# Writing p to DRAM straight from its 128x8 block on ScalarE's queue, in a two-layer graph attention kernel

## The chip, the cores and the metric

One core of one Trainium2 chip runs the kernel in one launch. The metric is the device time of a run in microseconds (us). Beside it stands the span of the profiled execution: the time from its first to its last instruction. The engines are TensorE (PE, with its weight loads as PEld), VectorE (DVE), ScalarE (ACT), GpSimd (POOL) and SyncE (SP, which only issues transfers here).

## The reference, cut to what matters

There are 16 graphs ("batches") of 1,024 nodes with 256 features, and a 0/1 matrix `adj` for each. Two layers follow each other. The second one needs, for each node, a few numbers that are shared with all other nodes:

```
# layer 0
x = layernorm(x + sigmoid(where(adj==1, leaky((x*a0) @ x.T), -inf)) @ x + bias)
# layer 1
Hh = x @ W;  s = Hh @ a_src;  d = Hh @ a_dst
e  = where(adj != 0, exp(-leaky_relu(s[:,None] + d[None,:])), 0)
x  = layernorm(x + elu((e @ Hh) / rowsum(e)))
```

The kernel does not compute `e` by an exponential for each pair of nodes. It makes exponentials for each node, p and q, and one VectorE instruction then makes a row tile of weights as min(p of the column times q of the row, adj). For that, q is wanted with one number per partition, as it comes, and p is wanted as a row of 1,024 numbers that is the same on all 128 partitions. p arrives in the other shape: `pq_kept[:, 0:8]`, 128 partitions by 8 tiles of nodes. Turning the one shape into the other is what is changed here.

## The kernel before, in words

A batch is handled in eight tiles of 128 nodes. The loop `for b in range(1, B)` works on layer 0 of batch b and on layer 1 of batch `prev` = b - 1 at the same time, and finishes the norm of batch `done` = b - 2. There is no scheduler that moves instructions: each engine executes its instructions in the order in which they are written, and a wait on an engine holds up all that is written behind it on that engine.

The first part of the loop body is a loop over eight strips (`jt`). In each of them

- `strip(b, jt)` makes the scores of the strip's nodes with the nodes at or right of them: TensorE matmuls into `pe` (L254), two tanh on ScalarE (L262, L263), a maximum on VectorE (L264). `finish` (L270) writes the result into `al`. Scores left of the diagonal are not computed, since the score matrix is symmetric.
- `dump(b, jt)` turns the strip by VectorE's 32x32 transposes (L290) and writes it to DRAM with four transfers on SP's queue (L294, `mir<-tb`). `gather(b, t)` reads strip t back, mirrored, into `al` (L298, `al<-mir`). In SP's queue they stand in this order: dump 0, dump 1, gather 0, dump 2, gather 1, dump 3, gather 2, gather 3, dump 4, dump 5, gather 4, dump 6, gather 5, gather 6. `mask(b, t, ...)` multiplies what gather t has brought by `adj` on VectorE (L305).
- `project(prev, t)` makes H and the numbers p and q of one tile of nodes of the batch before: two matmuls (L582), then on ScalarE three small exponentials and products; the third of them (L594) writes the tile's columns of `pq_kept`. The larger copy of H out of PSUM (L603) is put off until the next tile, and `evict_H` does the last one. Tiles 6 and 7 are projected in strip 4.

In strip 5 the products of layer 0 begin. They follow Strassen's scheme with seven half-size products (L477). `product(b, 1)` is put ahead of strip 5's scores and needs only unmirrored parts. `product(b, 5)`, four matmul steps ahead of strip 6's scores, needs the top left quarter of `al`, mirrored, masked and combined. VectorE prepares it in this order: mask 0 and combine rows 0 and 1 (written in strip 4); then in strip 5 mask 1 and combine row 2 (`combine_al(b, 1, 2, 3)`, L455), the lower halves of masks 0 and 1, mask 2 and combine row 3 (`combine_al(b, 1, 3, HT)`). Each of the four steps of the product reads one of the four rows. After the strips come products 3, 6, 7, 2 and 4, then the weights of the batch before (L643, `e`) and its sums (L648).

`share_p(prev)` stands in strip 5 right behind `product(b, 1)`. TensorE transposes the 128x8 block into PSUM (L610), ScalarE copies the 8x128 result to SBUF (L612), GpSimd's queue writes it to DRAM in eight runs of 512 B (L614, `p_row<-row`), and the same queue, after that has landed, reads it back to all 128 partitions (L616, `p<-p_row`). Behind these on GpSimd is `center` of batch `done` (L338 to L374), whose results `mr` and `r` ScalarE needs for scaling `y_kept` (L379).

The last batch is done in two halves by `share_half`: VectorE transposes `pq_kept` by 32x32 blocks (L624), GpSimd's queue writes four transfers (L628) and reads the half back (L629).

Transfers tell their landing by semaphores. The built program has eight of them for the transfers that SP and ScalarE issue, given out in rotation over both queues, in an order that the builder makes of the engines' lists and that is not the order of time on the chip, and eight others for GpSimd's. A transfer whose semaphore is still out waits on its own queue until the earlier transfer with the same semaphore has landed.

Of the kernel before, what the change touches and what calls it, by code (L numbers as in the profile page):

```python
# [9 lines left out]
F32 = mybir.dt.float32  # L10
# [8 lines left out]
P = 128  # L19
HALF = 512  # L20
BIG = 1.0e30
SLOPE = 0.2
SQ = 32
# [7 lines left out]
def one_kind_pass(  # L31
# [33 lines left out]
    nc = tc.nc  # L65
    B, N, D = x.shape
    NT = N // P
    ND = D // P
    HT = HALF // P
# [6 lines left out]
    one = ctx.enter_context(tc.tile_pool(name="one", bufs=1))  # L76
    two = ctx.enter_context(tc.tile_pool(name="two", bufs=2))
    dram = ctx.enter_context(tc.tile_pool(name="dram", bufs=2, space=bass.MemoryType.DRAM))
# [521 lines left out]
    def evict_H():  # L600

        for H, acc, wr in unscaled:
            nc.scalar.mul(H, acc, wr)  # L603
        unscaled.clear()

    def share_p(b):


        pt = ps_t.tile([P, HT, P], F32, tag="t", name=f"prow_{b}")[0:NT, 0, :]
        nc.tensor.transpose(pt, pq_kept[:, 0:NT], ident)  # L610
        row = one.tile([NT, P], F32, tag="row", name=f"row_{b}")
        nc.scalar.copy(row, pt)  # L612
        p_row = dram.tile([N], F32, tag="p_row", name=f"p_row_{b}")
        nc.gpsimd.dma_start(p_row.rearrange("(t p) -> t p", p=P), row)  # L614
        p_bcs[b] = one.tile([P, N], F32, tag="p", name=f"p_{b}")
        nc.gpsimd.dma_start(p_bcs[b], p_row.partition_broadcast(P))  # L616

    def share_half(b, t0):


        if t0 == 0:
            p_bcs[b] = one.tile([P, N], F32, tag="p", name=f"p_{b}")
        pT = one.tile([P, SQ], F32, tag="pT", name=f"pT_{b}_{t0}")
        nc.vector.transpose(pT, pq_kept)  # L624
        p_row = dram.tile([HALF], F32, tag="p_half", name=f"p_row_{b}_{t0}")
        v = p_row.rearrange("(t i j) -> i t j", i=P // SQ, j=SQ)
        for i in range(P // SQ):
            nc.gpsimd.dma_start(v[i], pT[ds(i * SQ + t0, HT), :])  # L628
        nc.gpsimd.dma_start(p_bcs[b][:, ds(t0 * P, HALF)], p_row.partition_broadcast(P))  # L629

    def check_pq(b):
        near = small.tile([P, 2, NT], F32, tag="near", name=f"near_{b}")
# [148 lines left out]
    for b in range(1, B):  # L781
        prev, done = b - 1, b - 2
        last = b == B - 1

        projects = [[0, 1], [2], [3], [4, 5], [6, 7], [], [], []]
        if prev == 0:

            projects = [[], [], [0, 1], [2, 3], [4, 5, 6, 7], [], [], []]
        for jt in range(NT):
            if jt == 4:  # L790
                mask(b, 0, 0, HT)
                combine_al(b, 1, 0, 2)
            if jt == 5:
                new_yT(b)
                product(b, 1)
                share_p(prev)
                mask(b, 1, 0, HT)
                combine_al(b, 1, 2, 3)
                mask(b, 0, HT)
                mask(b, 1, HT)  # L800
                mask(b, 2, 0, HT)
                combine_al(b, 1, 3, HT)
                mask(b, 2, HT)
                if done >= 0:
                    r1s[done] = center(mv1s[done], f"1_{done}", unit=1.0 / D)
            if jt == 6:
                unite(b, "p1")
                product(b, 5)
                unite(b, "p5")
                combine_al(b, 2, 0, HT)  # L810
            strip(b, jt)
            if jt == 5:
                mask(b, 3, HT)
            finish(b, jt, ends=False)
            if jt == 4:
                gather(b, 3)
            if jt < NT - 1:
                dump(b, jt)
            if jt < 2 and done >= 0:
                deviation1(done, NT - 2 + jt)  # L820
            if prev == 0 and jt == 0:
                turn_x1(0, 0)
            if prev == 0 and jt == 1:
                transpose_x1(0)
            if jt >= 1 and jt != 4:
                gather(b, jt - 1)
            if jt < 4 and b == 1:
                combine_x(b, jt)
            for t in projects[jt]:
                project(prev, t)  # L830
            if jt == 4:
                evict_H()
            add_twice(b, jt)
        if not last:
            new_xT(b + 1)
            load_blocks(xTs[b + 1], x[b + 1], 0, N)

        def extras(n):
            if prev == 0 and n < 2:
                scale0(0, HT + 2 * n)  # L840
                scale0(0, HT + 2 * n + 1)
            elif prev > 0:
                scale0(prev, 2 * n)
                scale0(prev, 2 * n + 1)
            if done >= 0:
                for q in (2 * n, 2 * n + 1):
                    scale1(done, q)
                    if q == 3:
                        store(done, 0, HT)
            if n < 3:  # L850
                check_adj(b, n)

        product(b, 3)
        combine_al(b, 3, 0, HT)
        extras(0)
        product(b, 6)
        weights(prev, 0)
        mask(b, 4)
        mask(b, 5)
        combine_al(b, 4, 0, 2)  # L860
        mask(b, 6)
        combine_al(b, 4, 2, HT)
        unite(b, "u2")
        extras(1)
        product(b, 7)
        extras(2)
        product(b, 2)
        extras(3)
        unite(b, "s")
        unite(b, "c12")  # L870
        unite(b, "c22")
        unite(b, "c11")
        product(b, 4)
        turn_y(b, 0)
        if done >= 0:
            store(done, HT, HT)
        weights(prev, 1)
        weights(prev, 2)
        weights(prev, 3)
        weights(prev, 4)  # L880
        unite(b, "c21")
        turn_y(b, 1)
        fetch_y(b, 0)
        fetch_y(b, 1)
        if not last:
            load_x(b + 1, [nc.sync])
        check_adj(b, 3)
        weights(prev, 5)
        weights(prev, 6)
        weights(prev, 7)  # L890
        check_pq(prev)
        if not last:
            load_adj(b + 1, 0, behind=x1s[b][:, HT, 0:1])

        def sum_of(t):
            homes = {"a": (ps_acc, "acc"), "e": (ps_e, "e"), "t": (ps_t, "t")}
            return acc1(prev, t, *homes[("aaeteeaa" if last else "aaeettat")[t]])

        n_first = 3
        first = [sum_of(t) for t in range(n_first)]  # L900
        for m in range(NT):
            for t in range(n_first):
                sum1(prev, t, first[t], m)
        if not last:
            turn_x(b + 1, 0, False)
            turn_x(b + 1, 1, False)
        rinvs = invert_sums(prev, first)
        for t in range(NT):
            if t >= n_first:
                acc = sum_of(t)  # L910
                for m in range(NT):
                    sum1(prev, t, acc, m)
            if last and t == 7:
                for m in range(4):
                    weights(b, m, 0, HT)
            elu(prev, t, *((first[t], rinvs[t]) if t < n_first else (acc,)))
            if last and t in (2, 3):
                for q in range(HT):
                    stats0(b, (t - 2) * HT + q)
                roots0(b, t - 2)  # L920
            if t >= 1:
                add(prev, t - 1)
            if t >= 2:
                deviation1(prev, t - 2)
            if not last and t in (3, 5):
                sums0(b, (t - 3) // 2)
                if t == 5:
                    load_adj(b + 1, 1, behind=mv0s[b][:, HT, 0:1])
            if not last and t >= 4:
                for q in range(2 * t - 8, 2 * t - 6):  # L930
                    deviation0(b, q)
                if t % 2 == 1:
                    roots0(b, (t - 5) // 2)
            for n in ([0], [1], [2, 3])[t - 5] if not last and t >= 5 else []:
                combine_x(b + 1, n)
            if t == 3 and not last:
                scale_x(b + 1, 0)
                scale_x(b + 1, 1)
            if last and t in (4, 6):
                t0 = (t - 4) // 2 * HT  # L940
                for n in range(HT):
                    project(b, t0 + n)
                evict_H()
                share_half(b, t0)
            if last and t in (5, 7):
                for q in range(HT):
                    scale0(b, (t - 5) // 2 * HT + q)
            if last and t == 7:
                for m in range(4, 6):
                    weights(b, m, 0, HT)  # L950
        if not last:
            add(prev, NT - 1)
# [522 lines left out]
```

## Time and profile before

| what | value |
|---|---|
| time, median of 3 runs | 1219.08 us (1217.61 to 1219.70) |
| profiled execution, its own time | 1218.96 us |
| its span | 1217.2 us |
| PE busy | 1206.9 us (99%), 4,400 matmuls |
| PEld, DVE, ACT, POOL busy | 67%, 82%, 70%, 32% |
| granted TensorE clock | 0.998 of full |
| transfers | 604,600 packets, 180.66 MB, 56.0% of the 16 engines' time by the queue that SP uses |

The profiled execution is 0.12 us under the median of the runs. Between two batches lie 74.4 us. A busy share is a share of the whole span; a wait names the instruction that waited, and behind the arrow what released it. "Landing" is the time at which a transfer's semaphore was raised.

### The profile page before, as it was taken

How to read it: one execution, taken by the hardware profiler on the slowest of the kernel's cores; microseconds unless marked ns; L12 is line 12 of the kernel's file. 1: busy time of each engine (PE TensorE's matmuls, PEld its weight loads, DVE VectorE, ACT ScalarE, POOL GpSimd, SP SyncE). 2: the span in 40 equal slices, each digit the busy share in tenths (PEclk: the TensorE clock that was granted, in tenths of full speed). 3: DMA queues.
4: the chain of work that ended last, by engine and by line, in shares of the span. 5: the costliest groups of instructions: out<-in, count | busy, mean ns of one | idle time of the engine just before them, and what ended most of it. 6: DMA issues, size and time to landing. Idle time of an engine off the chain costs nothing.

```text
span 1217.2 us, 15868 instructions
## 1 busy us (share of the span) xinstructions
PE 1206.9 (99%) x4400; PEld 819.4 (67%) x4400; DVE 993.4 (82%) x1759; ACT 846.5 (70%) x2150; POOL 391.2 (32%) x730
## 2 busy tenths in 40 slices
PE   9999999999999999999999999999999999999997
PEld 6757657576575866758667585775757657576686
DVE  5698797887969789797897978879798796887957
ACT  4574867767687676867768677786776867577674
POOL 3320333404243142441414324143340433404243
PEclk9999999999999999999999999999999999999999
DMA  9568787797878878788787886877769787887512
GB/s 195 104 133 153 130 158 154 148 184 137 154 152 155 180 136 160 145 166 172 142 171 132 156 179 132 176 139 143 173 143 189 128 156 151 156 182 137 112 52 73
DMA packets 604600, 180.66 MB, mean 148 GB/s; under 512 B 482012, under 2 KB 586968, under 8 KB 604504
## 3 DMA queue, kind: packets, MB, share of 16 engines
q1 hardware_dynamic: 582800, 136.90, 56.0%
q0 software_dynamic: 21008, 42.01, 18.8%
q8 instruction: 37, 0.61, 0.2%
q10 hardware_dynamic: 696, 0.66, 0.2%
q14 instruction: 59, 0.48, 0.1%
HBM read 152.44 MB, written 60.62 MB: 175 GB/s over the span
## 4 chain that ended last, share of the span: by engine, by line
PE 96%; ACT 2%; DVE 1%; POOL 1%; DMA 0%; issue 0%; ACTq 0%; DVEq 0%; POOLq 0%
PE acc L648 36%; PE pe L254 20%; PE pH L582 9%; PE pQ L477 8%; PE pV L477 8%; PE pW L477 8%; PE pR L477 4%; PE acc L396 2%; ACT junk L130 0%; ACT y_kept L379 0%; DMA p_row<-row 0%; PE busy L149 0%; PE pal L313 0%; ACT x L379 0%; POOL ve L338 0%
## 5 line engine op out<-in xcount | busy, mean ns | idle before, releaser
L648 PE MATMUL acc<-H,e 128*128 128x257 f32 x2032 | 445.6, 380 | 0.6 <-DVE e L643 0.6
L648 PEld LDWEIGHTS acc<-H,e 128*128 128x128 f32 x2032 | 384.8, 190 | 64.8 <-issue 7.2
L254 PE MATMUL pe<-xa,xT 128*128 128x384 f32 (+1 forms) x720 | 249.5, 486 | 0.2 <-DVE xa L235 0.2
L254 PEld LDWEIGHTS pe<-xa,xT 128*128 128x128 f32 x720 | 132.8, 190 | 90.0 <-issue 50.7
L284 POOL TENSOR_TENSOR al<-ident,al 128x128 f32<-128x128 f32 x128 | 103.7, 818 | 198.6 <-DVE al L270 198.5
L643 DVE SCALAR_TENSOR_TENSOR e<-p,pq_kept,adj 128x1024 f32<-128x1024 f32 (+1 forms) x136 | 159.2, 1224 | 0.0
L455 DVE TENSOR_TENSOR al<-al 128x1024 f32<-128x1024 f32 (+2 forms) x105 | 144.9, 1380 | 11.7 <-POOL al L284 4.5
L264 DVE TENSOR_TENSOR tb<-tb,low 128x512 f32<-128x512 f32 (+1 forms) x192 | 104.7, 551 | 39.8 <-ACT low L263 39.7
L262 ACT ACTIVATE tb<-pe 128x512 f32<-128x512 f32 (+1 forms) x192 | 93.8, 489 | 59.4 <-PE pe L254 57.7
L130 ACT ACTIVATE junk<-adj,minus 128x2048 bf16<-128x2048 bf16 x64 | 127.3, 1990 | 0.0
L582 PE MATMUL pH<-Wx,yT 128*128 128x258 f32 x480 | 116.3, 380 | 0.0
L104 POOL CAST adj<-x 128x1 bf16<-128x1 f32 x15 | 3.2, 212 | 348.9 <-DMA x<-y_rows 298.4
L582 PEld LDWEIGHTS pH<-Wx,yT 128*128 128x128 f32 x480 | 91.2, 190 | 31.1 <-issue 13.4
L477 PE MATMUL pV<-al,S 128*128 128x512 f32 x240 | 107.9, 592 | 0.0
L477 PE MATMUL pW<-al,x 128*128 128x512 f32 x240 | 107.9, 592 | 0.0
L477 PE MATMUL pQ<-al,x 128*128 128x512 f32 x240 | 107.9, 592 | 0.0
L270 DVE SCALAR_TENSOR_TENSOR al<-tb,adj 128x512 f32<-128x512 f32 (+7 forms) x132 | 97.4, 739 | 4.5
L305 DVE SCALAR_TENSOR_TENSOR al<-al,adj 128x512 f32<-128x512 f32 (+3 forms) x150 | 81.6, 564 | 18.6 <-DMA al<-mir 18.1
L263 ACT ACTIVATE low<-pe 128x512 f32<-128x512 f32 (+1 forms) x192 | 94.1, 490 | 1.2 <-DVE tb L264 1.2
L379 ACT ACTIVATE y_kept<-y_kept,mr,r 128x256 f32<-128x256 f32 x120 | 64.9, 588 | 42.9 <-POOL mr L374 41.7
L674 ACT ACTIVATE sums<-acc,tiny 128x1 f32<-128x1 f32 x45 | 11.7, 261 | 111.0 <-PE acc L648 111.0
L684 DVE TENSOR_SCALAR rinv<-acc 128x1 f32<-128x1 f32 x82 | 12.8, 157 | 89.9 <-PE acc L648 89.8
(152 smaller groups left out, 1681.7 us busy)
## 6 DMA issues: line engine op xcount, KB each, us to landing
adj<-in_adjT POOLq DMA_DIRECT2D x30, 1024.0 KB, 8.4
x<-in_x SPq DMA_DIRECT2D x15, 1024.0 KB
y_rows<-Z SPq DMA_DIRECT2D x240, 64.0 KB, 2.0
x<-y_rows SPq DMA_DIRECT2D x30, 512.0 KB, 4.3
out<-y_kept SPq DMA_DIRECT2D x30, 512.0 KB, 3.0
xT<-in_x SPq DMA_DIRECT2D x112, 128.0 KB, 4.0
p<-p_row POOLq DMA_DIRECT2D x15, 512.0 KB, 4.2
mir<-tb SPq DMA_DIRECT2D x60, 112.0 KB, 3.0
```

The costliest lines, as they stand in the source:

```text
L130: nc.scalar.activation(junk, rows, AF.Square, bias=minus1, scale=2.0, accum_out=chk[:, b * CHECKS + n : b * CHECKS + n + 1],)
L254: nc.tensor.matmul(pe[:, 0:w], lhsT=xTs[b][:, c, ts(jt, P)], rhs=xas[b][:, c, ds(jt * P + o, w)], start=(c == 0), stop=(c == ND - 1),)
L262: nc.scalar.activation(tb[:, ds(o, w)], pe[:, 0:w], AF.Tanh, scale=0.5)
L263: nc.scalar.activation(low[:, 0:w], pe[:, 0:w], AF.Tanh, scale=0.5 * SLOPE)
L264: nc.vector.tensor_tensor(tb[:, ds(o, w)], tb[:, ds(o, w)], low[:, 0:w], ALU.max)
L270: nc.vector.scalar_tensor_tensor(als[b][:, jt, c0:c1], tbs[b, jt][:, c0 - jt * P : c1 - jt * P], 1.0, adjs[b, jt // HT][:, jt % HT, c0:c1] ...
L284: nc.gpsimd.tensor_tensor(diag, ident2, diag, ALU.add)
L455: nc.vector.tensor_tensor(out_, in0, in1, ALU.subtract)
L477: nc.tensor.matmul(banks[bank], lhsT=lhs[:, jt, :], rhs=rhs[:, jt, :], start=first and jt == 0, stop=jt == HT - 1, skip_group_check=True,)
L582: nc.tensor.matmul(pt, lhsT=x1Ts[b][:, c, ts(t, P)], rhs=Wx[:, c, :], start=(c == 0), stop=(c == ND - 1),)
L643: nc.vector.scalar_tensor_tensor(e, p_bcs[b][:, cols], q, rows, ALU.mult, ALU.min)
L648: nc.tensor.matmul(acc, lhsT=es[b][:, m, ts(t, P)], rhs=Hs[b][m], start=(m == 0), stop=(m == NT - 1),)
```

## The change

ScalarE writes p to DRAM itself, out of the 128x8 block, with one transfer in which every number is an element of its own: 1,024 elements of 4 B, since neighbours in a partition lie 512 B apart in DRAM. This stands in strip 4, between the exponentials of the last tile and the last copy of H. TensorE's transpose, ScalarE's copy and GpSimd's write go. GpSimd's read back to all partitions keeps its place. In the last batch the two halves are written in the same way, 512 elements each, and VectorE's transpose and the four writes of each half go.

```diff
-    def share_p(b):
-        pt = ps_t.tile([P, HT, P], F32, tag="t", name=f"prow_{b}")[0:NT, 0, :]
-        nc.tensor.transpose(pt, pq_kept[:, 0:NT], ident)
-        row = one.tile([NT, P], F32, tag="row", name=f"row_{b}")
-        nc.scalar.copy(row, pt)
-        p_row = dram.tile([N], F32, tag="p_row", name=f"p_row_{b}")
-        nc.gpsimd.dma_start(p_row.rearrange("(t p) -> t p", p=P), row)
-        p_bcs[b] = one.tile([P, N], F32, tag="p", name=f"p_{b}")
-        nc.gpsimd.dma_start(p_bcs[b], p_row.partition_broadcast(P))
-
-    def share_half(b, t0):
+    p_rows = {}
+
+    def save_p(b, t0, n):
+        p_rows[b, t0] = dram.tile([n * P], F32, tag=f"p_row_{n}", name=f"p_row_{b}_{t0}")
+        with nc.allow_non_contiguous_dma(reason="a column per tile of nodes"):
+            nc.scalar.dma_start(
+                p_rows[b, t0].rearrange("(t p) -> p t", p=P), pq_kept[:, ds(t0, n)]
+            )
+
+    def share_p(b, t0, n):
         if t0 == 0:
             p_bcs[b] = one.tile([P, N], F32, tag="p", name=f"p_{b}")
-        pT = one.tile([P, SQ], F32, tag="pT", name=f"pT_{b}_{t0}")
-        nc.vector.transpose(pT, pq_kept)
-        p_row = dram.tile([HALF], F32, tag="p_half", name=f"p_row_{b}_{t0}")
-        v = p_row.rearrange("(t i j) -> i t j", i=P // SQ, j=SQ)
-        for i in range(P // SQ):
-            nc.gpsimd.dma_start(v[i], pT[ds(i * SQ + t0, HT), :])
-        nc.gpsimd.dma_start(p_bcs[b][:, ds(t0 * P, HALF)], p_row.partition_broadcast(P))
+        nc.gpsimd.dma_start(
+            p_bcs[b][:, ds(t0 * P, n * P)], p_rows[b, t0].partition_broadcast(P)
+        )
...
             if jt == 5:
                 new_yT(b)
                 product(b, 1)
-                share_p(prev)
+                share_p(prev, 0, NT)
...
             for t in projects[jt]:
                 project(prev, t)
             if jt == 4:
+                save_p(prev, 0, NT)
                 evict_H()
...
                 for n in range(HT):
                     project(b, t0 + n)
+                save_p(b, t0, HT)
                 evict_H()
-                share_half(b, t0)
+                share_p(b, t0, HT)
```

## The prediction

> **What bounds the kernel now.** I read the page first, then the waits, then one steady batch (6) engine by engine in the timeline, then the transfers. From the page, the engines' busy time and the chain that ended last:
>
> ```profile
> PE 1206.9 (99%) x4400; PEld 819.4 (67%) x4400; DVE 993.4 (82%) x1759; ACT 846.5 (70%) x2150; POOL 391.2 (32%) x730
> PE 96%; ACT 2%; DVE 1%; POOL 1%; DMA 0%; issue 0%; ACTq 0%; DVEq 0%; POOLq 0%
> ```
>
> TensorE is the bound. A change gains only what it takes from TensorE's own list, and loses whatever makes TensorE wait. From the waits, by engine:
>
> ```profile
> POOL p L616 <- DMA p_row<-row: 40.5, 15, 3.7
> ACT row L612 <- PE prow L610: 28.0, 15, 2.1
> DVE al L305 <- DMA al<-mir: 18.1, 18, 1.6
> PEld acc L648 <- DVE e L643: 2.1, 4, 1.0
> ```
>
> The path of p is made of waits (lines 1 and 2), but on engines that aren't the bound. VectorE waits for gathers (line 3), so it has no time in hand before strip 5's masks. TensorE's own losses are four short stalls (line 4). Now batch 6, the timelines of PE, ACT and POOL:
>
> ```profile
> 451.23 0.27 PE L610 MATMUL prow<-ident,pq_kept 128*8 128x128 f32 x1
> 451.34 1.46 PE L254 MATMUL pe<-xa,xT 128*128 128x384 f32 x4
> 452.63 3.60 PE L477 MATMUL pV<-al,S 128*128 128x512 f32 x8
> ...
> 448.72 0.25 ACT L594 ACTIVATE pq_kept<-pH,rcol 128x2 f32<-128x2 f32 x1
> 448.86 0.83 ACT L603 ACTIVATE H<-pH,wr 128x256 f32<-128x256 f32 x2
> ...
> 452.09 0.63 POOL L614 DMA_DIRECT2D p_row<-row  x1 [1.56 <-ACT row L612]
> 455.50 0.57 POOL L616 DMA_DIRECT2D p<-p_row  x1 [2.79 <-DMA p_row<-row]
> ```
>
> The transpose holds TensorE from 451.23 to 451.34. The p numbers are complete at 448.97 (448.72 + 0.25). The same batch on SP's queue and on VectorE:
>
> ```profile
> 446.54 0.44 SPq L298 DMA_DIRECT2D al<-mir  x1
> 447.03 2.26 SPq L294 DMA_DIRECT2D mir<-tb  x4
> 449.70 2.59 SPq L298 DMA_DIRECT2D al<-mir  x2
> ...
> 450.53 0.38 DVE L305 SCALAR_TENSOR_TENSOR al<-al,adj 128x256 f32<-128x256 f32 x1
> 453.23 0.29 DVE L305 SCALAR_TENSOR_TENSOR al<-al,adj 128x128 f32<-128x128 f32 x1 [0.31 <-DMA al<-mir]
> 453.62 0.69 DVE L455 TENSOR_TENSOR al<-al 128x512 f32<-128x512 f32 x1
> ```
>
> Gather 1 leaves at 446.54, dump 3 behind it, gathers 2 and 3 from 449.70. Mask 1 runs at 450.53. Mask 2 starts at 453.23, at once when gather 2 has landed, and "combine row 3" at 453.62. The fourth step of product 5 begins at 455.21 (452.63 and six of eight records at 0.43). So gather 2 has under a microsecond (455.21 - 453.62 - 0.69 = 0.90) before TensorE waits.
>
> **What is removed.** TensorE loses 15 transposes. Each takes 0.109 us from its start to the next matmul's: 15 x 0.109 = 1.64 us off the bound. ScalarE loses 15 copies (0.26 each), beside its wait. GpSimd loses 15 issues of 0.63 us and, in the last batch, eight of 0.52, and VectorE two transposes of 0.21; none of these is on the path. PSUM gets one buffer back, for which nobody waited.
>
> **What is added on ScalarE.** One issue per batch. ScalarE's issues at the start and end of this trace took 0.24 to 0.57 us. It stands before the last H copy, after which ScalarE idles 1.85 us (waiting for the transpose that goes) and 1.04 us more, so I cost it at nothing; over 2.9 us it would delay strip 5's tanh. In the last batch the two issues have 0.36 and 0.20 us of idle behind them: 0 to 0.3 us in all.
>
> **How long the write takes.** Nothing in this trace writes single numbers. By packets: mirror writes of 16 KB land in 1.5 us, y rows of 512 packets in 2.0, loads of 1,024 packets in 4.0 (medians of the transfer list), the slowest mirror write in 5.3. I take 2.5, nearest to the y rows and a little over them for twice the packets, and keep 1.5 to 5.3.
>
> ```profile
> y_rows<-Z SPq DMA_DIRECT2D x240, 64.0 KB, 2.0
> xT<-in_x SPq DMA_DIRECT2D x112, 128.0 KB, 4.0
> al<-mir SPq DMA_DIRECT2D x15, 384.0 KB, 3.7
> al<-mir SPq DMA_DIRECT2D x15, 320.0 KB, 3.4
> ```
>
> [...]
>
> **What is moved: the wait that decides.** The write stands on a queue that shares semaphores with SP. The built program of the changed kernel, with waits (batch 3; its second and third write of dump 1, the gather of strip 1, the new write's reader on GpSimd):
>
> ```
> L294 DMACopy mir_1_1770<-tb_1_1753 32x24x32 [waits DMAHW0_49]
> L294 DMACopy mir_1_1770<-tb_1_1753 32x24x32 [waits DMAHW2_49]
> L298 DMACopy al_1711<-mir_1_1770 128x6x128 [waits DMAHW3_49,DMAHW2_49,DMAHW1_49]
> L620 DMACopy p_1903<-p_row_0_1893 128x1024 [waits DMAHW1_49,DMASW1_49]
> ```
>
> The rotation skips from semaphore 0 to 2 because number 1 went to p_row, which the builder put among dump 1's writes though ScalarE reaches it only in strip 4. Gather 1 is the next to use number 1, so it waits for p_row to land. I followed the counts: it is so in each of batches 2 to 15; in batch 1 it is the second write of dump 3 that waits. Behind gather 1 on SP stand dump 3, gathers 2 and 3, dump 4 and the rest.
>
> The sum for a steady batch: p complete 448.97, write issued about 449.2, landed 451.7. Gather 1 leaves at 451.7 instead of 446.54. Gather 2 follows 3.16 later as before (449.70 - 446.54): 454.86, and lands after the 3.5 us that it took in this batch (449.70 to 453.20): 458.36. Mask 2 and combine row 3 end 0.39 + 0.69 later: 459.44. TensorE, 0.11 earlier without the transpose, wants the fourth step at 455.10. Stall: 4.34 us. Gather 1's own landing (451.7 + 3.7 = 455.4) and the masks fed by it are done in that time. Gather 3 leaves when dump 3 has landed, as now 2.2 us after gather 2: 457.1, landed 460.2, just ahead of mask 3. Further on VectorE is 5.1 us later and TensorE 4.3, so its lead shrinks by 0.8; before products 6 and 7 it has 1.7 and 1.3 us, before the sums 0.5 to 1.5 in a good batch, so nothing or little is added.
>
> Batch 1: the p numbers are complete at 76.64, the write lands at 79.4, three writes of 0.5 and gather 2 with 3.2 us follow, then 1.1 of VectorE: 85.4 where TensorE wants 83.0, 2.4 us.
>
> **What goes the other way.** GpSimd waits 2.7 us per batch for p_row, and `center` behind it is what makes ScalarE and then the weights late; TensorE's stalls there sum to 1.55 us. p_row now lands some 3 us earlier for GpSimd, so I let them go.
>
> Sum against the profiled execution's 1218.96: 14 x 4.34 = 60.8, + 2.4, - 1.64, - 1.55 = +60.0: 1279 us. The median of the runs is 0.12 higher, which changes nothing.
>
> **Rivals.**
> 1. *Faster: the shared semaphore doesn't hold.* Only the transposes and the stalls count: 1218.96 - 1.64 - 1.55 = 1215.8. For it: the diff touches neither SP nor its data. Against it: p doesn't exist before 448.97. It decides the sign where gather 1 may leave by about 447.4 (455.1 - 1.08 - 3.5 - 3.16), 1.5 us before that. 3%.
> 2. *The write of single numbers is slow.* At 5.3 us the stall is 7.1: 1318. At 8 us it is 9.8: 1356. For it: no row of the trace shows such a write. 10%.
> 3. *TensorE's clock falls as well.* In this trace the clock was granted in full only 3.5 us after the first matmul and halved 3.6 us after the last. The stall comes in two parts with a step of 0.86 us between them, 2.4 us and less, so I think not; if it fell for some 3.5 us in each batch, 14 x 1.7 = 24 us more: 1303. 10%.
> 4. *Half of it is absorbed.* With SP's queue idle before, the gathers land a microsecond sooner and the write in 1.5: 4.34 - 2 = 2.3 a batch: 1250. 10%.
>
> **How the numbers follow.** The forecast has 67%: 1265 (write 1.5) to 1300 (write 4.0). From 1250 to 1318 it takes in cases 3 and 4 and the near edge of 2, and leaves out the rest, under 2 in 10. About 0.2% (2.4 us) is what a measurement of this kernel can tell from no change. All cases but the first are far above it: slower 0.95, faster 0.03, the same 0.02 for a stall that the slack swallows.
>
> **What would show it.** Right: SP's gather waits for p_row about 14 times, some 5 us each; VectorE's wait for `al<-mir` grows from 18 to 70 us or more; the weight loads of `pV` wait for VectorE's L455 in each batch; PE falls to about 94%, and batches lie 78.7 us apart instead of 74.4; GpSimd's wait for p_row shrinks. Wrong: batches 74.3 apart and gather 1 ahead of p_row's landing (case 1); p_row landing after more than 5 us (case 2); half clock in the middle of the run (case 3); waits on ScalarE behind its own issue (a cost that I put at nothing).

## The result, and the profile after

| | before | after |
|---|---|---|
| time, median (6 runs each) | 1218.61 us | 1449.59 us (1446.05 to 1452.94) |
| ratio, 95% interval | | 1.1896 (1.1875 to 1.1918) |
| profiled execution, its span | 1217.2 us | 1446.2 us |
| batches apart (product 1 to product 1) | 74.4 to 75.3 us | 87.0 to 91.5 us |
| granted TensorE clock | 0.998 | 0.925 |

The direction was right and the size was not: +231 us where +60 was forecast. From the page of the changed kernel, the engines' busy time and the chain that ended last:

```profile
PE 1261.1 (87%) x4385; PEld 841.1 (58%) x4385; DVE 992.4 (69%) x1757; ACT 845.3 (58%) x2135; POOL 347.1 (24%) x707
PE 74%; DMA 16%; ACT 4%; SPq 3%; DVE 2%; issue 1%; DVEq 0%; ACTq 0%
```

TensorE is no longer the only bound: transfers hold 16% of the chain, where they held 0%. PE's busy time *grew* by 54 us although 15 transposes went. The same matmuls ran longer, which points at the clock. The waits, of the engines and then of SP's queue (total us, times, longest):

```profile
DVE al L305 <- DMA al<-mir: 222.0, 43, 12.7
PEld pV L477 <- DVE al L455: 204.7, 29, 10.9
POOL p L620 <- DMA p_row<-pq_kept: 140.5, 16, 11.5
```

```profile
SPq L298 <- DMA p_row<-pq_kept: 168.6, 14, 13.5
```

Read them from the last to the first: SP's gather waits for the new write, 14 times, 12 us each. VectorE waits for the gather, TensorE for VectorE. The mechanism is the predicted one, more than twice as long. Batch 6 (the matmul behind product 1 starts at 522.01) in the timelines of ScalarE, SP and PE:

```profile
519.77 0.37 ACTq L612 DMA_DIRECT2D p_row<-pq_kept  x1
```

```profile
513.00 0.43 SPq L298 DMA_DIRECT2D al<-mir  x1
528.32 0.38 SPq L298 DMA_DIRECT2D al<-mir  x1
532.37 4.17 SPq L298 DMA_DIRECT2D al<-mir  x2
```

```profile
534.45 2.07 PE L477 MATMUL pV<-al,S 128*128 128x512 f32 x2 [9.27 <-DVE al L455]
538.24 2.08 PE L477 MATMUL pV<-al,S 128*128 128x512 f32 x2 [1.72 <-DVE al L455]
```

The write is issued at 519.77 and lands 8.5 us later, at 528.30 (over the batches 8.3 to 10.9; the median in the transfer list is 9.7). Gather 1 leaves 0.02 us after that. TensorE loses 9.27 and 1.72 us. Two matmuls take 2.07 us, where four took 1.88 at 523.30. They run at half clock, as the stretches show (PE, PEld, DVE, ACT, POOL busy, then PEclk, DMA share, GB/s):

```profile
525.00:530.00 5.00, 0.18 (x1) 0.00 (x0) 0.00 (x0) 0.00 (x0) 0.98 (x3) 0.87 0.05 11
530.00:535.00 5.00, 0.55 (x1) 0.50 (x2) 1.73 (x4) 0.00 (x0) 2.77 (x7) 0.50 0.94 252
540.00:545.00 5.00, 5.00 (x15) 3.21 (x14) 4.86 (x9) 3.52 (x9) 1.01 (x3) 0.76 0.31 66
```

The clock is 0.50 from 528.7 to 542.4 and costs TensorE time after its data has come. Up to the last matmul it is halved for 211.6 us. The first of these rows also shows what the waiting looks like on the chip: 5 us in which the transfer engines are busy to 5% and move 11 GB/s.

### The profile page after: what moved, and what is told of

It is laid out like the page before. It is cut to its first block, busy times and chain, and to the rows that moved or that the text cites. A ratio compares the mean times of both kernels' runs of the same rounds, so it can differ in the third digit from the quotient of the medians.

```text
span 1446.2 us, 15798 instructions
## 1 busy us (share of the span) xinstructions
PE 1261.1 (87%) x4385; PEld 841.1 (58%) x4385; DVE 992.4 (69%) x1757; ACT 845.3 (58%) x2135; POOL 347.1 (24%) x707
## 4 chain that ended last, share of the span: by engine, by line
PE 74%; DMA 16%; ACT 4%; SPq 3%; DVE 2%; issue 1%; DVEq 0%; ACTq 0%
PE acc L641 29%; PE pe L254 17%; DMA p_row<-pq_kept 11%; PE pW L477 7%; PE pV L477 6%; PE pH L582 6%; DMA al<-mir 5%; PE pR L477 4%; PE pQ L477 4%; SPq L294 3%; PE acc L396 2%; DVE al L455 1%; ACT wr L593 1%; ACT tb L262 1%; ACT low L263 0%
## 5 line engine op out<-in xcount | busy, mean ns | idle before, releaser
L477 PE MATMUL pV<-al,S 128*128 128x512 f32 x240 | 147.4, 743 | 170.2 <-DVE al L455 170.2
L254 PE MATMUL pe<-xa,xT 128*128 128x384 f32 (+1 forms) x720 | 265.4, 513 | 0.0
L305 DVE SCALAR_TENSOR_TENSOR al<-al,adj 128x512 f32<-128x512 f32 (+3 forms) x150 | 76.4, 525 | 222.3 <-DMA al<-mir 222.0
L254 PEld LDWEIGHTS pe<-xa,xT 128*128 128x128 f32 x720 | 147.6, 210 | 102.9 <-issue 60.6
L477 PEld LDWEIGHTS pV<-al,S 128*128 128x128 f32 x240 | 50.8, 233 | 240.1 <-DVE al L455 204.7
L284 POOL TENSOR_TENSOR al<-ident,al 128x128 f32<-128x128 f32 x128 | 94.4, 738 | 342.8 <-DVE al L270 342.7
L636 DVE SCALAR_TENSOR_TENSOR e<-p,pq_kept,adj 128x1024 f32<-128x1024 f32 (+1 forms) x136 | 160.0, 1230 | 11.6 <-DMA p<-p_row 11.6
L495 ACT COPY yT<-pV 128x512 f32<-128x512 f32 x15 | 8.8, 586 | 236.7 <-PE pV L477 236.7
```

The lines of the kernel that those rows point to most:

```text
L254: nc.tensor.matmul(pe[:, 0:w], lhsT=xTs[b][:, c, ts(jt, P)], rhs=xas[b][:, c, ds(jt * P + o, w)], start=(c == 0), stop=(c == ND - 1),)
L284: nc.gpsimd.tensor_tensor(diag, ident2, diag, ALU.add)
L477: nc.tensor.matmul(banks[bank], lhsT=lhs[:, jt, :], rhs=rhs[:, jt, :], start=first and jt == 0, stop=jt == HT - 1, skip_group_check=True,)
L636: nc.vector.scalar_tensor_tensor(e, p_bcs[b][:, cols], q, rows, ALU.mult, ALU.min)
```

## The experiments

All times are medians, each beside runs of the kernel before on the same chip (1218.05 to 1219.24 us). e4 and e10 ask for landing times alone and have no row. In e2, e5, e7 and e8 the numbers of p do not reach their places, so these runs tell of time alone.

| run | time, us | ratio (95%) |
|---|---|---|
| e1: element write on GpSimd's queue | 1340.99 | 1.1009 (1.0991 to 1.1028) |
| e5: the same, numbers 64 B apart | 1219.62 | 1.0016 (1.0002 to 1.0030) |
| e3: before, and an unrelated write | 1254.63 | 1.0299 (1.0282 to 1.0317) |
| e7: after, numbers 64 B apart | 1332.36 | 1.0943 (1.0924 to 1.0961) |
| e2: after, runs of 32 B | 1314.46 | 1.0794 (1.0742 to 1.0846) |
| e8: e2 with p read back later | 1273.47 | 1.0439 (1.0414 to 1.0464) |
| e6: GpSimd's queue, runs of 32 B | 1296.62 | 1.0645 (1.0627 to 1.0663) |
| e9: turned by VectorE | 1230.25 | 1.0093 (1.0079 to 1.0107) |
| e11: e6, put in order by GpSimd | 1235.82 | 1.0139 (1.0124 to 1.0155) |
| e12: before, centre first | 1219.55 | 1.0008 (0.9999 to 1.0017) |

### Is it the queue or the write? (e1, e5)

e1 moves the write to GpSimd's queue, whose semaphores SP does not share:

```diff
-            nc.scalar.dma_start(
+            nc.gpsimd.dma_start(
                 p_rows[b, t0].rearrange("(t p) -> p t", p=P), pq_kept[:, ds(t0, n)]
```

> The changed kernel with the element write on GpSimd's queue instead of ScalarE's, in the same place (and in the last batch's halves). GpSimd's transfers have their own semaphores, so SP's gather of strip 1 no longer waits for it; the 1,024 elements of 4 B stay. Theory (shared semaphore times a slow write): gathers leave where they left before the change, at about -4.7 us from the end of product 1; p lands late and may cost VectorE and the weights 0 to 3 us a batch: 1217 to 1260 us, full clock. Rival (the element write itself clogs the transfer engines or the way to DRAM for all others): gather 1 lands as late as in the changed kernel and the time stays above 1350 us.

Neither time held. SP no longer waits for p_row, and gathers 1 and 2 leave where they left before the change, but the time is still 123 us over the kernel before. From the transfer lists (KB each, median us to landing), the kernel before and then e1:

```profile
al<-mir SPq DMA_DIRECT2D x15, 256.0 KB, 3.0
```

```profile
al<-mir SPq DMA_DIRECT2D x15, 256.0 KB, 10.0
p_row<-pq_kept POOLq DMA_DIRECT2D x15, 4.0 KB, 10.4
```

The gather of 256 KB on *SP's* queue, which leaves while the write is under way, took 3.0 us in the kernel before and takes 10.0 here. So a write of 4 KB that lands late seems to hold up another queue's transfers with it. e5 tests that by the addresses (one DRAM buffer serves all its batches):

```diff
...
+                p_rows[b, t0][0 : n * P * 16].rearrange("(t p s) -> p t s", p=P, s=16)[:, :, 0:1],
+                pq_kept[:, ds(t0, n)].rearrange("p (t s) -> p t s", s=1),
...
```

> As the run with the write on GpSimd's queue, but neighbouring numbers stand 64 B apart in DRAM (still 1,024 elements of 4 B; the read back takes the first 4 KB, so the weights of layer 1 are not the reference's). Theory: it is elements that share a line of DRAM that are slow, and while they are, they hold up the other transfers (mirror gathers took up to 11 us in the run before this one). Then the write lands about 2.5 us after its issue, gather 2 lands after some 3.5 us as before the change, and the time is 1215 to 1225 us. Rival: any write of 1,024 single elements holds up the others, or GpSimd's own lateness is what cost 122 us: 1290 to 1345 us.

```profile
al<-mir SPq DMA_DIRECT2D x15, 256.0 KB, 3.7
p_row<-pq_kept POOLq DMA_DIRECT2D x15, 4.0 KB, 4.5
```

The theory's time held: the same 1,024 elements on the same queue, 64 B apart, cost 1.6 us (0.2 to 3.7) where side by side they cost 123, and the gather lands in 3.7 us. The write itself lands in 4.5 us, not in the 2.5 that were expected. It was the neighbourhood in DRAM that was slow, not the count of elements.

### The place in the rotation alone (e3)

The kernel before, with a write that has nothing to do with p, in eight runs of 512 B, where the change has its own:

```diff
             if jt == 4:
+                other = dram.tile([N], F32, tag="other", name=f"other_{b}")
+                nc.scalar.dma_start(other.rearrange("(t p) -> t p", p=P), ident[0:NT, :])
                 evict_H()
```

> The kernel before, with its path of p untouched, and one more write on ScalarE's queue at the place where the change puts its own: eight runs of 512 B of a constant to a DRAM buffer that nobody reads. It moves nothing that is needed; it only takes a place in the rotation of semaphores. Theory: SP's gather 1 waits for it in 14 batches; landing in about 2 us, the stall is 3.3 to 3.9 us a batch: 1262 to 1275 us. Rival (an idle transfer costs nothing; the loss comes from p's own path): 1217 to 1222 us.

```profile
SPq L298 <- DMA other<-ident: 45.6, 14, 3.6
```

SP's gather waits 14 times for a transfer whose data nobody reads: +36 us. The rival is out. The price is under the expected 43 to 56; TensorE's stalls of over 0.7 us sum to 27.9 us, and its clock fell once. (A stall is counted as what the distance between the starts of two matmuls has over the usual one.)

### The form of the write (e4, e10)

Both add 16 writes to the end of the kernel before, each behind the one before it, in two rounds of eight forms. In e4:

```diff
+            nc.scalar.dma_start(bench[0:N].rearrange("(t p) -> p t", p=P), pq_kept[:, 0:NT])
+            nc.scalar.dma_start(bench[0:HALF].rearrange("(t p) -> p t", p=P), pq_kept[:, 0:HT])
+            nc.scalar.dma_start(bench[0:N].rearrange("(p t) -> p t", p=P), pq_kept[:, 0:NT])
...
```

> The kernel before, and behind its last store on ScalarE's queue sixteen writes to one DRAM buffer, each waiting for the one before: twice through eight forms (8 runs of 512 B; 1,024 elements of 4 B that lie as in the change; 512 of these; 128 runs of 32 B; 1,024 elements 64 B apart; 1,024 elements 512 B apart; 1,024 runs of 64 B; 1,024 runs of 128 B). Only their landing times count, not the kernel's time, which grows by their sum. [...] Theory B (neighbours in one line of DRAM disturb each other): only the form of the change is slow, elements 64 or 512 B apart land in 2 to 4 us. Theory C (it is the traffic of the batch that makes it slow): all land in 2 to 3 us here.

With nothing beside them, from issue to landing in the two rounds: the change's write 8.50 and 10.91 us; half of it, 512 elements, 9.08 and 10.09; 128 runs of 32 B 1.44 and 1.44; 1,024 elements 64 B apart 2.51 and 2.59, and 512 B apart 2.56 and 2.45; 1,024 runs of 64 B 2.15 and 2.14, and of 128 B 2.26 and 2.77. That is theory B: it is not the batch's traffic, not the count, and not 4 B as such. e10 asks for the spacing:

```diff
+            nc.scalar.dma_start(bench[0:P].rearrange("(t p) -> p t", p=P), pq_kept[:, 0:1])
...
+            nc.scalar.dma_start(bench[0 : N * 4].rearrange("(t p s) -> p t s", p=P, s=4)[:, :, 0:1], cols)
...
```

> The kernel before with 16 more writes at its end on ScalarE's queue, one waiting for the other, eight forms in two rounds: single numbers side by side, 128, 256 and 1,024 of them (neighbours from neighbouring partitions); 1,024 of them 8, 16, 32 and 64 B apart; 1,024 of them 8 B apart whose neighbours come from the same partition. Theory (numbers that share a line of DRAM and come at the same time disturb each other): 1,024 side by side 8 to 11 us as before and 64 B apart 2.5 us; the time falls with the spacing and is gone at the length of a line, at 32 or 64 B; already 128 numbers side by side take several us, since 1,024 took no longer than 512. Rival (a fixed price of the transfer's own list of elements): 8, 16 and 32 B apart all take 2.5 us like 64 B, and 128 side by side take 2 us.

ScalarE's timeline in e10; each write is issued when the one before has landed, so the distance of two starts is the landing time of the upper one:

```profile
1212.26 1.07 ACTq L1096 DMA_DIRECT2D bench<-pq_kept  x1
1220.47 0.38 ACTq L1097 DMA_DIRECT2D bench<-pq_kept  x1
1229.71 0.38 ACTq L1098 DMA_DIRECT2D bench<-pq_kept  x1
1239.14 0.37 ACTq L1099 DMA_DIRECT2D bench<-pq_kept  x1
1244.61 0.37 ACTq L1100 DMA_DIRECT2D bench<-pq_kept  x1
1247.64 0.37 ACTq L1101 DMA_DIRECT2D bench<-pq_kept  x1
1250.58 0.37 ACTq L1102 DMA_DIRECT2D bench<-pq_kept  x1
1253.15 0.59 ACTq L1103 DMA_DIRECT2D bench<-pq_kept  x1
1259.23 0.33 ACTq L1096 DMA_DIRECT2D bench<-pq_kept  x1
```

| form (line) | numbers within 64 B | us, two rounds |
|---|---|---|
| 128, side by side (L1096) | 16 | 8.2, 7.3 |
| 256, side by side (L1097) | 16 | 9.2, 10.9 |
| 1,024, side by side (L1098) | 16 | 9.4, 9.3 |
| 1,024, 8 B apart (L1099) | 8 | 5.5, 4.2 |
| 1,024, 16 B apart (L1100) | 4 | 3.0, 3.9 |
| 1,024, 32 B apart (L1101) | 2 | 2.9, 2.6 |
| 1,024, 64 B apart (L1102) | 1 | 2.6, 2.6 |
| 1,024, 8 B apart, neighbours from one partition (L1103) | 8 | 6.1, 6.3 |

The theory held in every row, and the rival in none that tells them apart. The more single numbers fall into the same 64 B, the longer the landing; the effect is gone at 32 or 64 B apart (these rows do not tell the two apart), and 512 B apart is no faster (e4). 128 side by side cost nearly what 1,024 cost. Neighbours from one partition are no better than from many.

### The terms of the sum (e7, e2, e8)

e7 gives the changed kernel the landing that the prediction assumed, by e5's addresses on ScalarE's queue.

> As the changed kernel (ScalarE's queue, the same place, the same semaphores), but neighbouring numbers stand 64 B apart in DRAM (the weights of layer 1 are not the reference's). It makes the landing that the prediction assumed, 2.5 us. If the prediction's sum is right but for that term, the time is 1279 us. Theory now: the sum also lacks TensorE's clock, and the broadcast of p that runs beside gathers 1 and 2: 1.1 us a batch later than with runs of 32 B (1314 us), with the clock some 1330 to 1350 us.

1332.36 us with a landing of 2.7: the theory's range. The step from e7 to the changed kernel, 117 us, is the price of the slow landing and of what follows from it. The other 53 us between 1279 and 1332 are terms that the sum lacked. TensorE's stalls of over 0.7 us sum to 83.6 us in its trace, where the prediction's 4.34 x 14 + 2.4 gives 63; matmuls outside the stalls, above all at half clock, took about 32 us longer than usual.

e2 keeps ScalarE's queue and writes 128 runs of 32 B:

```diff
-                p_rows[b, t0].rearrange("(t p) -> p t", p=P), pq_kept[:, ds(t0, n)]
+                p_rows[b, t0].rearrange("(p t) -> p t", p=P), pq_kept[:, ds(t0, n)]
```

> The changed kernel with one difference: in DRAM p lies node by node of a partition, so that ScalarE's write has 128 runs of 32 B instead of 1,024 elements of 4 B (the reader takes the numbers in the wrong order, so the output is not the reference's; all later work is the same). Same queue, place, semaphore and wait. Theory: the write lands in about 2.5 us, the gather leaves some 5 us late instead of 11, TensorE stalls about 4.3 us a batch in two parts, the clock stays full: about 1279 us (1265 to 1300), the sum of the prediction with its own landing time. Rival (the wait costs the same whatever the write's form, since the gather is held by something else): 1430 to 1450 us.

The write lands in 1.4 us. 1314.46 us lies between the two, above the theory's 1300 and far below the rival, and the clock did not stay full: it fell 15 times. Compared with e7 the run gains 17.9 us, 1.28 us for each of 14 batches, which is about the landing's own 1.3 (the runs of e2 spread from 1308 to 1322). But it stays 60 us above e3, whose gather 1 leaves only 0.7 us earlier. In e2 GpSimd reads p back right behind the write, beside gathers 1 and 2, and gather 2 (320 KB) takes 4.7 us instead of 3.4. e8 reads p back later:

```diff
...
-                share_p(prev, 0, NT)
...
             if jt == 4:
                 save_p(prev, 0, NT)
                 evict_H()
+            if jt == 6:
+                share_p(prev, 0, NT)
```

> As the run with 128 runs of 32 B on ScalarE's queue (the weights of layer 1 are not the reference's), but GpSimd reads p back in strip 6, behind the sum of strip 6's diagonal, instead of in strip 5. Theory: in the run before, the 512 KB broadcast ran beside gather 2, which took 4.6 to 5.6 us from issue to landing instead of 3.5; without it gather 2 lands some 1.3 us sooner, TensorE's stalls and its halved clock shrink: 1265 to 1295 us instead of 1314. Rival: the broadcast is not what lengthens gather 2: 1305 to 1322 us.

Gather 2 in e2, then in e8:

```profile
al<-mir SPq DMA_DIRECT2D x15, 320.0 KB, 4.7
```

```profile
al<-mir SPq DMA_DIRECT2D x15, 320.0 KB, 3.4
```

The theory held: 1273.47 us, the stalls at 37.1 us instead of 60.7 and the half clock at 37.5 us instead of 78.5. The broadcast of p beside the gathers cost 41 us, the clock included.

### Is there a better version? (e6, e9, e11, e12)

e6 keeps all that was to be gained: GpSimd's queue, runs of 32 B, no transpose. p then stands in another order, and VectorE reads it with a stride:

```diff
...
+        ps = p_bcs[b][:, cols].rearrange("q (p t) -> q t p", p=P)
+        e, rows = (v.rearrange("q (t p) -> q t p", p=P) for v in (e, rows))
+        nc.vector.scalar_tensor_tensor(e, ps, q, rows, ALU.mult, ALU.min)
```

> p is written on GpSimd's queue in 128 runs of 32 B (the 8 numbers of a partition side by side), and VectorE reads the broadcast row with a stride of 8 numbers in the weights (L636). Theory: no slow write, no place among the semaphores of SP and ScalarE, no transposes: the prediction's case 1, 1215.8 us, 1213 to 1222 with what the stride and the earlier broadcast may cost. Rival: a strided operand slows the 136 instructions of the weights on VectorE (1.28 us each now) by a half or more, or the broadcast beside gathers 2 and 3 delays them: 1230 to 1290 us.

The rival's first half held. Strip 5 runs as in the kernel before (gather 2 lands at the same time), and the loss is in the weights, from VectorE's groups by form:

```profile
L638 DVE SCALAR_TENSOR_TENSOR e<-p,pq_kept,adj 128x1024 f32<-128x1024 f32 x120 | 241.9, 2070 | 0.0
```

2070 ns each instead of the 1288 of the kernel before: a stride of 32 B on one of three operands cost 0.78 x 120 = 94 us of VectorE. No other stride was tried.

e11 has GpSimd put p in order, once per batch:

```diff
...
+        nc.gpsimd.tensor_copy(
+            to.rearrange("q (t p) -> q t p", p=P), raw.rearrange("q (p t) -> q t p", p=P)
+        )
...
```

> As the run with 128 runs of 32 B on GpSimd's queue, but VectorE reads no stride: the broadcast lands in a row of the weights' tile that is written last, and GpSimd puts the 1,024 numbers into order with one copy per batch behind strip 7, where it waits for other things. Theory: strip 5 was undisturbed in the run with the stride, so this keeps the removed transposes (15 x 0.109 us) and costs nothing on the path: 1214 to 1219 us. Rival: GpSimd's strided copy takes several us, so that the first weights are late, or it slows VectorE beside it: 1221 to 1245 us.

The rival held. The copy takes 2.04 us and comes 2.6 us late for the first weights, 16 times (41.5 us of VectorE's waits): +17 us. e9 lets VectorE turn the block in every batch, as it did in the last:

```diff
             if jt == 4:
                 evict_H()
+                share(prev, 0, NT)
...
```

> The kernel before, with p turned in every batch as it was turned in the last one: VectorE transposes the block by 32x32 at the end of strip 4, GpSimd's queue writes it in four transfers with runs of 128 B and reads it back. No transpose on TensorE, no copy on ScalarE, nothing on the semaphores of SP and ScalarE, no run under 128 B, no stride on VectorE's side. Theory: this keeps what the change was worth and nothing of what it cost: 15 transposes of 0.109 us and up to 1.5 us of stalls behind GpSimd's late centre, 1215 to 1218 us. Rival: 0.21 us more on VectorE per batch, four issues of 0.52 us on GpSimd ahead of the read and of the centre, and the broadcast beside gathers 2 and 3 eat it: 1218 to 1226 us.

Worse than the rival's range: +11 us. Counted from the end of product 1, the read back of p leaves at +4.5 us (before: +4.1), and `center` behind it begins at +7.5 us instead of +4.7 and takes 6.4 us instead of 4.7; why it takes longer stays open. ScalarE's wait for `mr` goes from 41.7 to 81.3 us, and the weight loads of the sums (`acc`) wait 11.0 us for the weights where they waited 2.1.

e12 takes up the prediction's credit of 1.55 us, by putting `center` ahead of the read back on GpSimd:

```diff
...
-                share_p(prev)
+                p_row = share_p(prev)
...
                     r1s[done] = center(mv1s[done], f"1_{done}", unit=1.0 / D)
+                spread_p(prev, p_row)
```

> The kernel before, but on GpSimd the centre of batch done stands ahead of the read back of p instead of behind it. It tests the prediction's term of 1.55 us for TensorE's four stalls behind ScalarE's late scaling. If the late centre makes them, they go: 1217.0 to 1218.2 us, and ScalarE's wait for the centre's result shrinks; if something else makes them, the time is that of the kernel before, 1218.5 to 1220 us.

ScalarE's wait for `mr` falls from 41.7 to 6.7 us, and the time is the same (1.0008, 0.9999 to 1.0017). But the read back now comes later, and VectorE waits for p, which it did not before:

```profile
DVE e L647 <- DMA p<-p_row: 11.7, 9, 2.0
```

So the swap was worth nothing; since it traded one delay for another, it does not tell what the late centre alone costs. No version tried here beats the kernel before.

## Why the prediction was wrong

**Which queue, which wait, who stands behind it: right.** SP's gather waits for p_row 14 times, and each wait passes on to VectorE and TensorE. e3 shows this step by itself, at 36 us.

**"How long the write takes. I take 2.5, and keep 1.5 to 5.3": the step that failed.** It measured 9.7 (8.3 to 10.9). The bounds came from transfers with many packets, and the count of packets was the wrong property. 1,024 elements do land in 2.6 us if they stand 64 B apart (e10; 2.7 in e7); none of the rows used had single numbers side by side. The 1,040 packets of the batch 6 write start within 0.68 us in the trace, so the count is indeed cheap; the 7 us come after that, before the landing. The kernel's own p write in its last batch, runs of 128 B in 1.6 us, was no guide either.

**Rival 2 had the right mechanism, "at 8 us, 1356".** Its condition was met, but it too was priced without its company. The prediction's own formula at 9.7 gives 4.34 + 7.2 = 11.5 us x 14 = 161, with 9.6 in batch 1 (which the rival had left at 2.4), less 3.2 of savings: 1386. Missing from it:

- **Rival 3, the clock, came true together with rival 2.** The prediction took them for alternatives. The stalls were expected as two of "2.4 us and less", too short for the clock to fall. The matmuls took about 41 us longer outside the stalls than usual, against about 2 in the kernel before: 39 us, or 36 if the smallest excesses are counted too. Even e8, with no stall over 2.72 us, loses its clock 10 times.
- **"After the 3.5 us that it took in this batch": gather 2 took 4.7.** The read back of p starts when the write lands, which is when the held gathers start. 1.2 x 14 = 17 us. The prediction followed p to GpSimd, but not its 512 KB into the gathers' way.
- **The last batch, "0 to 0.3 us": about 6.** From batch 15's product 1 to the end of the span lie 115.4 us instead of 94.6, and 14.4 of the 20.8 more have arisen by the end of strip 5's `product(b, 5)`. Behind it VectorE waits 11.6 us for the two halves of p. The prediction priced the two issues and forgot the landing.
- **Savings of 1.64 and 1.55 us.** The second was to come from p_row landing "some 3 us earlier for GpSimd". It landed later: the read back leaves 7.5 us after product 1 instead of 4.1. Nor did e12, with the centre first, show any gain. The first is seen in e5 (74.31 us between most batches instead of 74.42), but the run's time is not lower.

1386.4 + 39.1 + 16.8 + 6 + 3.2 = 1451.5, against 1448.1 for the profiled execution. So close a meeting is partly luck, since some of the clock's 39 us lies between the two stalls of a batch, where TensorE would have waited anyway. The path itself comes out well: over the fifteen batches TensorE reaches the fourth step 188 us later than before, where the formula with gather 2's term gives 161 + 9.6 + 16.8 = 187, less 1.6 for the transposes. By differences between runs alone: 36 us for the place in the rotation (e3), 19 more where gather 1 leaves 0.7 us later, for what follows from it and for whatever else differs (e8), 41 for the broadcast beside the gathers (e2), 18 for a landing of 2.7 instead of 1.4 (e7), 117 for 9.7. The clock is inside each of these.

**Issue on ScalarE at nothing: right.** 0.37 us each, and nothing waits behind it. **"GpSimd's wait for p_row shrinks": wrong**, 40.5 to 140.5 us. Two small slips changed nothing: batch 1's parts add up to 85.2, not 85.4, and behind the second issue of the last batch ScalarE had 2.50 us of idle, not 0.20.

## What to carry to other kernels

Before a write is spread into single numbers, ask where neighbours land: 16 of them within 64 B cost some 7 us of landing here (9.4 against 2.6 in e10), and meanwhile a gather on another queue was held up too (10.0 us instead of 3.0 in e1), so another queue was no shelter. A transfer that is added to a queue takes a place in a rotation of semaphores, and here the one that came next in it waited for its landing, related or not (e3: 14 waits, 45.6 us in all, for data that nobody reads). When a held queue is let go, ask what else was waiting for the same event (the read back of p beside gather 2: 4.7 us in e2, 3.4 in e8 without it). The costs of a stall were not alternatives here: the transfer (9.7 us), the collision behind it (1.2 us a batch) and TensorE's clock (halved for 211.6 us) came together and belong in one sum.

## What the runs showed of the hardware

**Single numbers side by side.** e10's table above: 1,024 of them landed in 9.4 us side by side and in 2.6 us at 64 B apart. In e1 the slowness reached another queue, where the gather of 256 KB took 10.0 us instead of 3.0. Why numbers within the same 64 B hinder each other, and how another queue's transfer comes to wait with them, was not shown.

**TensorE's clock changed on a fixed grid.** In the changed kernel the clock falls at 262.48, 351.23, 439.97 and 528.72: steps of 88.74 or 88.75, which is 26 x 3.413. The stretches at half clock last 3.41 us or a multiple of it (3.4 in most batches of e8, 3.4 or 6.8 in e2, 6.8 in most of e7, 10.2 to 17.1 in the changed kernel). In each of the fourteen traces of this case every change of the clock lies on a grid of 3.413 us to within 3 ns. Cut into windows by this grid, with PE's idle time added up in each, the traces have 76 falls ahead of the last matmul, each behind a window with at least 1.77 us idle; where the clock stayed, a window had at most 2.00 us. Two stalls in one window counted together, as here in e8, a window with its neighbours:

```profile
545.00:549.68 4.68, 4.68 (x13) 2.08 (x11) 1.58 (x3) 1.66 (x4) 3.45 (x8) 1.00 0.64 137
549.68:553.09 3.41, 1.40 (x4) 0.37 (x3) 3.01 (x6) 0.00 (x0) 0.76 (x2) 1.00 0.75 193
553.09:556.50 3.41, 3.41 (x6) 2.07 (x7) 3.38 (x6) 0.58 (x1) 1.08 (x2) 0.50 0.28 44
```

Idle times of 0.61 and 1.41 us leave 1.40 us of work in 3.41, and the next window runs at 0.50 although PE is busy throughout (3.41 of 3.41 us). Of all the windows, one with 1.77 us idle was enough for a fall, and one with 2.00 us was not.
